# A Perceiver layer on one core: attention in six TensorE runs a group instead of eight, with the last 65 score columns two heads at a time

## The chip, the cores and the metric

The kernel runs on one core of a Trainium2 chip. The metric is the device time of one execution in microseconds; the median of three runs is given. The core has TensorE (matmuls and transposes, written PE in the profile; PEld is its loading of weights), VectorE (DVE), ScalarE (ACT), GpSimd (POOL) and SyncE (SP, which issues DMAs here). TensorE writes to PSUM, eight banks of 128 partitions x 512 words of four bytes; everything else lies in SBUF or in the chip's memory. All numbers are float32.

## The reference, cut to what matters

```python
# x: (16, 64, 1024), ctx_1024: (16, 1601, 256), mask: (64, 1601)
def xattn(q, k, v, mask):             # 32 heads of 32, 8 key/value heads, 4 heads to each
    xq = q.reshape(b, s, 8, 4, 32)
    xk = k.reshape(b, t, 8, 32)
    xv = v.reshape(b, t, 8, 32)
    scores = einsum('bsgrd,btgd->bgrst', xq, xk) / sqrt(32) + mask
    probs = softmax(scores, axis=-1)
    return einsum('bgrst,btgd->bsgrd', probs, xv).reshape(b, s, 1024)

x = x + xattn(layernorm(x), ctx, ctx, mask)
x = x + ffn_half_dropped(layernorm(x), w_gate, w_up, w_down)   # the smaller half of each row of silu(gate) is zeroed
x = x + experts_top2(layernorm(x), router_w, router_b, A, Bm)
```

The context of 1601 rows is both keys and values. The change touches the first of the three steps alone.

## The kernel before, in words

The 1024 rows of `x` are eight tiles of 128 rows (two batches each). The attention of one batch is cut into four groups (`Group(b, h, rh)`: half `h` of the key/value heads, that is four of them, and half `rh` of the four query heads to each). So a group has four heads `g`, one to each 32 partitions of the transposed keys `kT`, and in each head 128 rows (two query heads of 64 rows) against 1601 columns. There are 64 groups, worked off by one loop (`for n in range(ng)`), each in two halves `d`. All engines' instructions keep the order in which the loop issues them; the recorder that sees to it (`InOrder`, line 93) is why every row of the profile says L93, so rows are told apart by their tiles.

A group goes through these steps:

- `scores(c)` (TensorE): for part `c` of the columns, one matmul a head of 32 rows of `kT` with the queries `qt` as weights, into a bank a head (`ps`). The four heads lie in different 32-row strips of TensorE. The parts are `PARTS`: 289, 512, 288 and 512 columns. Heads 0 to 2 write to three banks of their own (`ps_s`), head 3 to one of the four banks of the pool `ps_t` (tag `pt`), which are handed out in rotation and shared with all transposes. A bank is taken anew when its last reader has finished.
- `masked(c)` (VectorE): one instruction a head adds the mask, writes the sum to `sc` in SBUF and leaves the maximum in `mx`; after the last part one reduction makes `nm`, the negated maxima of the four heads. A masked bank is free for the next scores.
- `softmax(g)` (ScalarE): the exponential of a head's 1601 columns, in place, with their sum.
- `turn(heads)` (TensorE): transposes of two heads' probabilities, 13 blocks of up to 128 columns each, four blocks to a bank `pt`; a head gives three banks of four blocks, and the last 65 columns of both heads share a bank, so a turn takes seven banks. `turn` returns the eight copies from `pt` to `pT`: the loop gives the first five to ScalarE, the sixth big one and the two small ones to VectorE.
- `values(c0, c1)` (TensorE): for blocks `c0` to `c1` of the columns, one matmul a head with `v` as weights, summed into one bank `po`; of the group before. `keep` copies `po` to `oT` and takes the reciprocals of the sums.

In a half `d` the loop issues, in this order: scores of a long part (512 columns) of the next group; the turn of two heads of this group; ScalarE's copies; the masks of the long part; VectorE's copies; scores and masks of a short part (288 or 289 columns) of the next group or the one after it; two exponentials; half of the values of the group before (six blocks, then seven). On TensorE each half is four runs of one kind of instruction, a group eight.

Around this stand a few steps that come once in eight groups (`m = n % 8`): the layer norm of the next 128 rows (`Norm.half`, `Norm.end` on VectorE, the power and `scaled_rows`, the normalised rows `xn`, on GpSimd), the turning of its queries (`turn_queries`, TensorE and ScalarE), and of finished outputs (`finish_tile`). GpSimd also makes one of 48 units of weight sums in a group (`sums_made`, `sums_out`, `sums_in`, tile `tw`), which the FFN uses. `load_kv(b + 1)` issues the next batch's keys and values on SP when the second group of batch `b` starts its scores.

Behind the attention the FFN and the experts are ordered by a planner that is not touched.

Of the kernel before, what the change touches and what calls it, by code (L numbers as in the profile page):

```python
# [9 lines left out]
F32 = mybir.dt.float32  # L10
# [6 lines left out]
ALU = mybir.AluOpType  # L17
AX = mybir.AxisListType
PSUM = bass.MemoryType.PSUM

P = 128
B, S, D = 16, 64, 1024
T, C = 1601, 256
HD = 32
NT = B * S // P
NTC = (T + P - 1) // P
TL = T - (NTC - 1) * P

PARTS = [(0, 289), (289, 801), (801, 1089), (1089, T)]
NCH = len(PARTS)  # L30
I = 2752
IC = 344
# [22 lines left out]
def tile_perceiver_layer(  # L55
# [22 lines left out]
    ident = const.tile([P, P], F32, name="ident")  # L78
# [18 lines left out]
    pe, dve, act = InOrder(nc.tensor), InOrder(nc.vector), InOrder(nc.scalar)  # L97
# [27 lines left out]
    early, late = ExitStack(), ExitStack()  # L125

    def new_pool(stack, name, bufs, side="left", space=bass.MemoryType.SB):
        return stack.enter_context(
            tc.tile_pool(name=name, bufs=bufs, side=side, space=space, reuse_waits="tile")
        )  # L130
# [3 lines left out]
    a1 = new_pool(early, "a1", 1)  # L134
    ktp = new_pool(early, "kT", 3)
    qtp = new_pool(early, "qT", 2)
    scp = new_pool(early, "sc", 2)
    xnp = new_pool(late, "xn", 1, "right")
    vp = new_pool(late, "v", 3, "right")
    ptp = new_pool(late, "pT", 8, "right")  # L140
    otp = new_pool(late, "oT", 2, "right")
    twp = new_pool(early, "tw", 3)
    xp = new_pool(late, "x", 3, "right")
# [1 line left out]
    ps_t = new_pool(early, "ps_t", 4, "right", PSUM)  # L145
# [40 lines left out]
    qT, kv, oT, rs_tok = {}, {}, {}, {}  # L186
# [25 lines left out]
    def scaled_rows(i, norm, engine):  # L212

        xn = xnp.tile([P, 2, 4, 4, HD], F32, tag="xn", name=f"xn{i}")
        xv = x[i].rearrange("p (h g r d) -> p h r g d", h=2, g=4, r=4)
        for h in range(2):
            engine.tensor_scalar(
                xn[:, h], xv[:, h], norm.mean, norm.rstd, ALU.subtract, ALU.mult
            )
        return xn  # L220

    def turn_queries(i, xn, h):

        if h == 0:
            qT[i] = qtp.tile([P, 2, 2, 4, S], F32, tag="qt", name=f"qt{i}")
        pt = ps_t.tile([P, 4, P], F32, tag="pt", name=f"ptq{i}_{h}")
        for r in range(4):
            pe.transpose(pt[:, r, :], xn[:, h, r].rearrange("p g d -> p (g d)"), ident)
        act.activation(
            qT[i][:, h].rearrange("p b r s -> p r b s"),  # L230
            pt.rearrange("p r (b s) -> p r b s", b=2),
            AF.Copy, scale=1.0 / math.sqrt(HD),
        )

    class Group:


        def __init__(self, b, h, rh):
            self.b, self.h, self.rh = b, h, rh
            self.name = f"{b}_{h}_{rh}"  # L240
            self.sc, self.pT = {}, {}

        def scores(self, c, spare=False):


            b, h, rh = self.b, self.h, self.rh
            if c == 0:
                self.sc = [
                    scp.tile([P, T], F32, tag=f"sc{g}", name=f"sc{g}_{self.name}")
                    for g in range(4)  # L250
                ]
                self.mx = small.tile([P, 4, NCH], F32, tag="mx", name=f"mx_{self.name}")
                self.sums = small.tile([P, 4], F32, tag="sums", name=f"sums_{self.name}")
                if (h, rh) == (0, 1) and b + 1 < B:
                    load_kv(b + 1)
            t0, t1 = PARTS[c]
            homes = [[(ps_s, f"ps{g}"), (ps_t, "pt")] for g in range(3)]
            homes.append([(ps_t, "pt"), (ps_o, "po")])
            self.ps = []
            for g in range(4):  # L260
                home, tag = homes[g][spare]
                ps = home.tile([P, 512], F32, tag=tag, name=f"ps{g}_{self.name}_{c}")
                self.ps.append(ps)
            for g in range(4):
                rows = slice(g * HD, (g + 1) * HD)
                q = qT[b // 2][rows, h, b % 2, 2 * rh : 2 * rh + 2, :]
                pe.matmul(
                    self.ps[g][:, : t1 - t0],
                    q.rearrange("p r s -> p (r s)"),
                    kv[b][0][h][rows, t0:t1],  # L270
                    start=True,
                    stop=True,
                )

        def masked(self, c, heads=range(4)):


            t0, t1 = PARTS[c]
            for g in heads:
                dve.tensor_tensor_reduce(  # L280
                    out=self.sc[g][:, t0:t1],
                    in0=self.ps[g][:, : t1 - t0],
                    in1=mask2[:, t0:t1],
                    scale=1.0,
                    scalar=LOWEST,
                    op0=ALU.add,
                    op1=ALU.max,
                    accum_out=self.mx[:, g, c : c + 1],
                )
            if c == NCH - 1 and 2 in heads:  # L290
                self.nm = small.tile([P, 4], F32, tag="nm", name=f"nm_{self.name}")
                dve.tensor_reduce(self.nm, self.mx, AX.X, ALU.max, negate=True)

        def softmax(self, g):

# [98 lines left out]
    ng = len(groups)  # L394
# [9 lines left out]
        pe.transpose(warm[:, 0, :], ident, ident)  # L404
    for h in range(2):
        turn_queries(0, xn, h)
    for group, c in [(groups[0], c) for c in range(NCH)] + [(groups[1], c) for c in range(2)]:
        group.scores(c, spare=c % 2 == 1)
        if c % 2 == 0:
            for _ in range(4):  # L410
                pe.transpose(group.ps[3][:, 3 * P :], ident, ident)
        group.masked(c)
    for g in range(2):
        groups[0].softmax(g)

# [2 lines left out]
    for n in range(ng):  # L418
        i, m = n // 8 + 1, n % 8
        group = groups[n]  # L420
        last = n == ng - 1
        if m == 2 and i < NT:
            load_x(i)
        if m == 4 and n > 8:
            sp_queue.dma_start(xs[i - 2], x[i - 2])
        if n == ng - 3:
            for j in range(2):
                x[j] = xp.tile([P, D], F32, tag="x", name=f"x{j}_f")
                sp_queue.dma_start(x[j], xs[j])
        for d in range(2):  # L430
            add = None
            long = (groups[n + 1], 2 * d + 1) if n + 1 < ng and n + d > 0 else None
            short = (groups[n + 1 + d], 2 - 2 * d) if n + 1 + d < ng else None
            if long:
                long[0].scores(long[1])
            if i < NT and d == 1 and m >= 6:
                turn_queries(i, xn, m - 6)
            if n > 8 and 3 <= 2 * m + d <= 4:
                copy, add = finish_tile(i - 2, 1 - d)
                act.copy(*copy)  # L440
            copies = group.turn((2 * d, 2 * d + 1))
            on_act = 3 if last else 5
            for copy in copies[:on_act]:
                act.copy(*copy)
            if long:
                long[0].masked(long[1], (3, 0, 1, 2))
            for copy in copies[on_act:]:
                dve.tensor_copy(*copy)
            if short:
                short[0].scores(short[1])  # L450
                short[0].masked(short[1])
            if d == 0:
                for g in (2, 3):
                    group.softmax(g)
            elif n + 1 < ng:
                for g in range(2):
                    groups[n + 1].softmax(g)
            if add:
                add()
            if n > 0:  # L460
                groups[n - 1].values(*((0, NTC // 2), (NTC // 2, NTC))[d])
                if d == 1:
                    groups[n - 1].keep()
            if i < NT:
                if (m, d) == (4, 0):
                    norm = Norm(x[i], f"q{i}")
                if (m, d) in ((4, 0), (5, 0)):
                    norm.half(m - 4)
                if (m, d) == (5, 1):
                    norm.end()  # L470
                    xn = scaled_rows(i, norm, pool)
            if d == 1 and 0 <= n - 3 < 3 * NU:
                sums_made(n - 3)
                sums_out(n - 3)
            if d == 1 and 0 <= n - 2 < 3 * NU:
                sums_in(n - 2)
            if last:
                xn = first[d].tile([P, D], F32, tag=("xn", "oT")[d], name=f"xn_f{d}")
                norm = Norm(x[d], f"f{d}")
                norm.half(0)  # L480
                norm.half(1)
                norm.end()
                dve.tensor_scalar(xn, x[d], norm.mean, norm.rstd, ALU.subtract, ALU.mult)
                first_xn[d] = xn
# [931 lines left out]
```

## Time and profile before

| | |
|---|---|
| median of three runs | 1723.66 us (1723.62 to 1723.87) |
| the profiled execution's own time | 1721.6 us |
| its span, first to last instruction | 1719.8 us |
| mean granted clock of TensorE | 0.997 |
| the attention's last values start | 837.72 us into the span |
| busy in 200 to 800 us, a group (46.5 groups) | 12.90 us of TensorE |

Busy time of an engine is the union of its instructions' times. A row of a timeline merges neighbours of one kind: it gives the start in us from the span's start, the busy time in us, the engine, what is written and read, the shape, how many instructions, and in brackets the idle time before it and what ended it. TensorE's matmuls overlap in its pipeline, so the time that a run takes is read from its start to the start of the next run, and not from its busy time. A float32 matmul on strips of the array is carried out as two instructions, so eight scores stand in a row for four heads.

### The profile page before, as it was taken

The page shows a single profiled execution, that of the slowest core. Times are in us where ns is not written, and L with a number is a line of the kernel's source. Part 1 is how long each engine was busy: PE and PEld are TensorE (multiplying, and loading weights), DVE is VectorE, ACT ScalarE, POOL GpSimd, SP SyncE. Part 2 cuts the span into 40 slices and gives each one's busy share as a digit, 9 for nine tenths or more (in the row PEclk, how much of TensorE's full clock was granted, in tenths as well). Part 3 has the DMA queues.
Part 4 walks back from the last instruction along what each step waited for, and adds up shares of the span by engine and source line. Part 5 has one row for each costly group of instructions (what it writes and reads, how often), then busy time and mean ns, then how long its engine had stood idle before and what let it go on. Part 6 is the DMA issues. An engine that isn't in the chain of part 4 may idle for free. (4 is left out here: it accounts for less than half of the span.)

```text
span 1719.8 us, 38753 instructions
## 1 busy us (share of the span) xinstructions
PE 1692.3 (98%) x15102; PEld 1151.8 (67%) x15102; DVE 1411.2 (82%) x3655; ACT 1260.8 (73%) x1780; POOL 558.6 (32%) x584
## 2 busy tenths in 40 slices
PE   8999999999999999999999999899999999999999
PEld 6777777777777777777766666446666546645644
DVE  7888888888888888888627999999989999999603
ACT  6999999999999999999544676676737874777010
POOL 2044453454544454110120221512250313332631
PEclk9999999999999999999999999999999999999999
DMA  8236456545556646211599999688989888888873
GB/s 248 85 112 221 144 194 213 186 170 191 172 173 212 204 159 203 70 61 58 193 333 326 307 291 311 210 297 308 301 278 305 266 300 269 285 291 275 317 265 141
DMA packets 132326, 384.56 MB, mean 224 GB/s; under 512 B 9488, under 2 KB 61232, under 8 KB 132144
## 3 DMA queue, kind: packets, MB, share of 16 engines
q1 hardware_dynamic: 113280, 312.83, 55.3%
q0 software_dynamic: 18432, 68.16, 11.7%
q8 instruction: 120, 1.97, 0.5%
q10 hardware_dynamic: 432, 1.09, 0.2%
q14 instruction: 62, 0.51, 0.1%
HBM read 339.58 MB, written 42.47 MB: 222 GB/s over the span
## 5 line engine op out<-in xcount | busy, mean ns | idle before, releaser
L93 DVE CUSTOM_DVE_ANT_0 sc<-ps,mask 128x512 f32<-128x512 f32 (+2 forms) x1024 | 526.3, 571 | 103.1 <-PE ps L93 102.7
L93 ACT ACTIVATE sign<-a,cand 128x2752 int8<-128x2752 f32 x136 | 351.9, 2588 | 107.8 <-DVE cand L93 107.3
L93 ACT ACTIVATE sc<-sc,nm 128x1601 f32<-128x1601 f32 x256 | 420.1, 1666 | 9.6 <-DVE nm L93 9.6
L93 PEld LDWEIGHTS pt<-ident,sc 128*128 128x128 f32 (+1 forms) x3328 | 361.9, 141 | 77.5 <-issue 72.8
L93 PE MATMUL pt<-ident,sc 128*128 128x128 f32 (+1 forms) x3328 | 391.1, 274 | 1.2 <-ACT sc L93 1.1
L93 DVE TENSOR_SCALAR_CACHE_REDUCE junk<-a,cand 128x2752 uint8<-128x2752 f32 x124 | 381.6, 3077 | 3.8
L93 ACT COPY pT<-pt 128x512 f32<-128x512 f32 x636 | 323.8, 607 | 46.2 <-PE pt L93 45.9
L93 PE MATMUL pg_g<-w_g,hS 128*128 128x344 f32 x896 | 263.9, 455 | 6.4 <-DVE s L93 3.3
L93 PE MATMUL pg_u<-w_u,hS 128*128 128x344 f32 x896 | 263.7, 452 | 0.0
L93 POOL TENSOR_TENSOR tw<-tw 128x344 f32<-128x344 f32 (+1 forms) x192 | 176.1, 928 | 267.0 <-DMA tw<-in_wd_dram 89.0
L93 PE MATMUL ps<-kT,qt 32*128 32x512 f32 (+2 forms) x2048 | 247.7, 549 | 3.1 <-DVE mx L93 2.8
L93 PEld LDWEIGHTS pg_g<-w_g,hS 128*128 128x128 f32 x896 | 170.0, 191 | 94.4 <-issue 4.2
L93 PE MATMUL pd<-w_d,s 128*128 128x512 f32 x528 | 231.0, 592 | 0.0
L93 PEld LDWEIGHTS pg_u<-w_u,hS 128*128 128x128 f32 x896 | 168.8, 190 | 86.8 <-issue 3.1
L93 PE MATMUL po<-pT,v 128*32 128x128 f32 x6656 | 208.1, 274 | 0.4 <-ACT oT L93 0.4
L93 PEld LDWEIGHTS po<-pT,v 128*32 128x32 f32 x6656 | 174.1, 110 | 48.6 <-issue 43.7
L93 PEld LDWEIGHTS pd<-w_d,s 128*128 128x128 f32 x528 | 98.6, 190 | 115.3 <-issue 114.8
L93 DVE COPY pT<-pt 65x128 f32<-65x128 f32 (+1 forms) x388 | 141.0, 418 | 23.0 <-PE pt L93 16.0
L93 PEld LDWEIGHTS ps<-kT,qt 32*128 32x128 f32 x2048 | 83.1, 183 | 52.2 <-DVE mx L93 34.8
L93 ACT ACTIVATE s<-s 128x344 f32<-128x344 f32 (+1 forms) x70 | 36.7, 537 | 91.3 <-DVE s L93 90.9
L93 POOL TENSOR_TENSOR s<-s,rank 128x688 f32<-128x688 f32 x32 | 62.4, 1967 | 88.2 <-DVE rank L93 87.4
L93 DVE DVE_READ_ACCUMULATOR2_ANT mx<- 128x1 f32 x1024 | 83.9, 82 | 0.0
(322 smaller groups left out, 1216.5 us busy)
## 6 DMA issues: line engine op xcount, KB each, us to landing
w_g<-ts SPq DMA_DIRECT2D x64, 688.0 KB
w_u<-ts SPq DMA_DIRECT2D x64, 688.0 KB
w_d<-ts SPq DMA_DIRECT2D x48, 768.0 KB
w_g<-in_wg_dram SPq DMA_DIRECT2D x48, 688.0 KB
w_u<-in_wu_dram SPq DMA_DIRECT2D x48, 688.0 KB
w_d<-in_wd_dram SPq DMA_DIRECT2D x36, 768.0 KB
kT<-in_ctx_t_dram SPq DMA_DIRECT2D x31, 800.5 KB
v<-in_ctx_v_dram SPq DMA_DIRECT2D x32, 768.0 KB
```

What stands on the lines that cost most here:

```text
L93: return tc.keep_in_program_order(getattr(self.engine, op)(*args, **kwargs))
```

## The change

The parts become three of 512 columns and one of 65. The 65 columns leave the rhythm of four heads: `rests` scores them two heads at a time, into banks of `ps_t`, just ahead of a 512-column part, so that they lie in the same run on TensorE. The first half of a group scores part 1 of the next group, turns heads 0 and 1, scores the rest of heads 0 and 1 and part 2, and then takes all values of the group before in one run; the second half scores the rest of heads 2 and 3 together with part 0 of the group after the next, and turns heads 2 and 3. TensorE thus has six runs a group. The maxima are reduced for two heads at a time (`maxima`), and the exponentials of the next group start one in each half. In the second half ScalarE gives one more big copy to VectorE (`on_act` is 5, then 4). VectorE masks head 3 first. `sc` gets a third buffer for heads 2 and 3, `pT` goes from eight buffers to six. The layer norm of the next rows and the turning of its queries move to earlier halves.

```diff
--- before.py
+++ after.py
@@ -26,7 +26,7 @@
 NTC = (T + P - 1) // P
 TL = T - (NTC - 1) * P
-PARTS = [(0, 289), (289, 801), (801, 1089), (1089, T)]
+PARTS = [(0, 512), (512, 1024), (1024, 1536), (1536, T)]
 NCH = len(PARTS)
 I = 2752
 IC = 344
@@ -134,10 +134,10 @@
     a1 = new_pool(early, "a1", 1)
     ktp = new_pool(early, "kT", 3)
     qtp = new_pool(early, "qT", 2)
-    scp = new_pool(early, "sc", 2)
+    scp = [new_pool(early, "sc", 2), new_pool(early, "sc_late", 3)]
     xnp = new_pool(late, "xn", 1, "right")
     vp = new_pool(late, "v", 3, "right")
-    ptp = new_pool(late, "pT", 8, "right")
+    ptp = new_pool(late, "pT", 6, "right")
     otp = new_pool(late, "oT", 2, "right")
     twp = new_pool(early, "tw", 3)
     xp = new_pool(late, "x", 3, "right")
@@ -238,22 +238,43 @@
         def __init__(self, b, h, rh):
             self.b, self.h, self.rh = b, h, rh
             self.name = f"{b}_{h}_{rh}"
-            self.sc, self.pT = {}, {}
+            self.sc, self.pT, self.rest = {}, {}, {}
+        def rests(self, heads):
+            for g in heads:
+                self.rest[g] = ps_t.tile(
+                    [P, 512], F32, tag="pt", name=f"rest{g}_{self.name}"
+                )
+                self.product(g, NCH - 1, self.rest[g])
+        def product(self, g, c, out):
+            b, h, rh = self.b, self.h, self.rh
+            t0, t1 = PARTS[c]
+            rows = slice(g * HD, (g + 1) * HD)
+            q = qT[b // 2][rows, h, b % 2, 2 * rh : 2 * rh + 2, :]
+            pe.matmul(
+                out[:, : t1 - t0],
+                q.rearrange("p r s -> p (r s)"),
+                kv[b][0][h][rows, t0:t1],
+                start=True,
+                stop=True,
+            )
         def scores(self, c, spare=False):
             b, h, rh = self.b, self.h, self.rh
             if c == 0:
                 self.sc = [
-                    scp.tile([P, T], F32, tag=f"sc{g}", name=f"sc{g}_{self.name}")
+                    scp[g // 2].tile([P, T], F32, tag=f"sc{g}", name=f"sc{g}_{self.name}")
                     for g in range(4)
                 ]
                 self.mx = small.tile([P, 4, NCH], F32, tag="mx", name=f"mx_{self.name}")
                 self.sums = small.tile([P, 4], F32, tag="sums", name=f"sums_{self.name}")
                 if (h, rh) == (0, 1) and b + 1 < B:
                     load_kv(b + 1)
-            t0, t1 = PARTS[c]
             homes = [[(ps_s, f"ps{g}"), (ps_t, "pt")] for g in range(3)]
             homes.append([(ps_t, "pt"), (ps_o, "po")])
             self.ps = []
@@ -261,25 +282,18 @@
                 home, tag = homes[g][spare]
                 ps = home.tile([P, 512], F32, tag=tag, name=f"ps{g}_{self.name}_{c}")
                 self.ps.append(ps)
             for g in range(4):
-                rows = slice(g * HD, (g + 1) * HD)
-                q = qT[b // 2][rows, h, b % 2, 2 * rh : 2 * rh + 2, :]
-                pe.matmul(
-                    self.ps[g][:, : t1 - t0],
-                    q.rearrange("p r s -> p (r s)"),
-                    kv[b][0][h][rows, t0:t1],
-                    start=True,
-                    stop=True,
-                )
-        def masked(self, c, heads=range(4)):
+                self.product(g, c, self.ps[g])
+        def masked(self, c, heads=(3, 0, 1, 2)):
             t0, t1 = PARTS[c]
             for g in heads:
+                ps = self.rest[g] if c == NCH - 1 else self.ps[g]
                 dve.tensor_tensor_reduce(
                     out=self.sc[g][:, t0:t1],
-                    in0=self.ps[g][:, : t1 - t0],
+                    in0=ps[:, : t1 - t0],
                     in1=mask2[:, t0:t1],
                     scale=1.0,
                     scalar=LOWEST,
@@ -287,9 +301,15 @@
                     op1=ALU.max,
                     accum_out=self.mx[:, g, c : c + 1],
                 )
-            if c == NCH - 1 and 2 in heads:
+        def maxima(self, j):
+            if j == 0:
                 self.nm = small.tile([P, 4], F32, tag="nm", name=f"nm_{self.name}")
-                dve.tensor_reduce(self.nm, self.mx, AX.X, ALU.max, negate=True)
+            heads = slice(2 * j, 2 * j + 2)
+            dve.tensor_reduce(
+                self.nm[:, heads], self.mx[:, heads], AX.X, ALU.max, negate=True
+            )
         def softmax(self, g):
@@ -404,12 +424,19 @@
         pe.transpose(warm[:, 0, :], ident, ident)
     for h in range(2):
         turn_queries(0, xn, h)
-    for group, c in [(groups[0], c) for c in range(NCH)] + [(groups[1], c) for c in range(2)]:
-        group.scores(c, spare=c % 2 == 1)
-        if c % 2 == 0:
-            for _ in range(4):
-                pe.transpose(group.ps[3][:, 3 * P :], ident, ident)
+    for j, (group, c) in enumerate(
+        [(groups[0], c) for c in range(NCH - 1)] + [(groups[1], 0)]
+    ):
+        if j == 2:
+            group.rests((0, 1))
+        group.scores(c, spare=j % 2 == 1)
+        if j == 2:
+            group.rests((2, 3))
         group.masked(c)
+        if j == 2:
+            group.masked(NCH - 1, range(4))
+            for half in range(2):
+                group.maxima(half)
     for g in range(2):
         groups[0].softmax(g)
@@ -427,47 +454,56 @@
             for j in range(2):
                 x[j] = xp.tile([P, D], F32, tag="x", name=f"x{j}_f")
                 sp_queue.dma_start(x[j], xs[j])
+        after = groups[n + 1 : n + 3] + [None, None]
         for d in range(2):
             add = None
-            long = (groups[n + 1], 2 * d + 1) if n + 1 < ng and n + d > 0 else None
-            short = (groups[n + 1 + d], 2 - 2 * d) if n + 1 + d < ng else None
-            if long:
-                long[0].scores(long[1])
-            if i < NT and d == 1 and m >= 6:
+            if i < NT and d == 0 and m >= 6:
                 turn_queries(i, xn, m - 6)
+            ahead, c = (after[0], 1) if d == 0 else (after[1], 0)
+            if d == 1 and after[0]:
+                after[0].rests((2, 3))
+            if ahead:
+                ahead.scores(c)
             if n > 8 and 3 <= 2 * m + d <= 4:
                 copy, add = finish_tile(i - 2, 1 - d)
                 act.copy(*copy)
             copies = group.turn((2 * d, 2 * d + 1))
-            on_act = 3 if last else 5
+            on_act = 3 if last else 5 - d
             for copy in copies[:on_act]:
                 act.copy(*copy)
-            if long:
-                long[0].masked(long[1], (3, 0, 1, 2))
+            if d == 1 and after[0]:
+                after[0].masked(NCH - 1, (2, 3))
+            if ahead:
+                ahead.masked(c)
+            if d == 1 and after[0]:
+                after[0].maxima(1)
             for copy in copies[on_act:]:
                 dve.tensor_copy(*copy)
-            if short:
-                short[0].scores(short[1])
-                short[0].masked(short[1])
             if d == 0:
                 for g in (2, 3):
                     group.softmax(g)
-            elif n + 1 < ng:
-                for g in range(2):
-                    groups[n + 1].softmax(g)
+                if after[0]:
+                    after[0].rests((0, 1))
+                    after[0].scores(2)
+                    after[0].masked(NCH - 1, (0, 1))
+                    after[0].masked(2, (0, 1))
+                    after[0].maxima(0)
+                    after[0].masked(2, (3, 2))
+                if n > 0:
+                    groups[n - 1].values(0, NTC)
+                    groups[n - 1].keep()
+            if after[0]:
+                after[0].softmax(d)
             if add:
                 add()
-            if n > 0:
-                groups[n - 1].values(*((0, NTC // 2), (NTC // 2, NTC))[d])
-                if d == 1:
-                    groups[n - 1].keep()
             if i < NT:
                 if (m, d) == (4, 0):
                     norm = Norm(x[i], f"q{i}")
-                if (m, d) in ((4, 0), (5, 0)):
-                    norm.half(m - 4)
-                if (m, d) == (5, 1):
+                if m == 4:
+                    norm.half(d)
+                if (m, d) == (4, 1):
                     norm.end()
+                if (m, d) == (5, 0):
                     xn = scaled_rows(i, norm, pool)
             if d == 1 and 0 <= n - 3 < 3 * NU:
                 sums_made(n - 3)
```

## The prediction

> **What bounds the kernel now.** I read the page, then the busy time by stretch, then the timelines of TensorE, ScalarE and VectorE over one group of the attention.
>
> ```profile
> core 0: us, PE busy (x) PEld busy (x) DVE busy (x) ACT busy (x) POOL busy (x), PEclk, DMA share, GB/s
> 400.00:600.00 200.00, 200.00 (x2958) 153.08 (x2956) 168.92 (x647) 185.70 (x306) 97.58 (x105) 1.00 0.58 190
> ```
>
> In the steady attention TensorE has no idle time at all, at full clock, while ScalarE (93%) and VectorE (84%) have a little. The chain of waits on the page runs back from the end through the FFN only, so it says nothing of this stage; the timeline does. Its columns are start, busy us, and the run.
>
> ```profile
> 500.12 1.14 PE L93 MATMUL ps<-kT,qt 32*128 32x512 f32 x8
> 501.19 3.06 PE L93 MATMUL pt<-ident,sc 128*128 128x128 f32 x26
> 504.17 0.77 PE L93 MATMUL ps<-kT,qt 32*128 32x289 f32 x8
> 504.87 1.74 PE L93 MATMUL po<-pT,v 128*32 128x128 f32 x56
> 506.54 1.14 PE L93 MATMUL ps<-kT,qt 32*128 32x512 f32 x8
> 507.61 3.06 PE L93 MATMUL pt<-ident,sc 128*128 128x128 f32 x26
> 510.60 0.77 PE L93 MATMUL ps<-kT,qt 32*128 32x288 f32 x8
> 511.30 1.52 PE L93 MATMUL po<-pT,v 128*32 128x128 f32 x48
> ...
> 837.72 3.05 PE L93 MATMUL po<-pT,v 128*32 128x128 f32 x104 [0.39 <-ACT oT L93]
> 840.70 1.09 PE L93 MATMUL pt_f<-ident,xn_f 128*128 128x128 f32 x8
> ```
>
> These are the eight runs of a group, back to back, with no wait between them: from start to start 1.07 + 2.98 + 0.70 + 1.67 + 1.07 + 2.99 + 0.70 + 1.45 = 12.63 us. (200 to 800 us holds 744 instructions of 512 columns, 16 a group, so 46.5 groups and 12.90 us each; the other 0.27 is the turning of queries and outputs.) So TensorE's own work sets the period, and all banks come free in time. How narrowly, the next two show: the copies out of the first turn (501.19), on ScalarE and on VectorE.
>
> ```profile
> 501.94 2.54 ACT L93 COPY pT<-pt 128x512 f32<-128x512 f32 x5 [0.44 <-PE pt L93]
> 504.33 1.67 ACT L93 ACTIVATE sc<-sc,nm 128x1601 f32<-128x1601 f32 x1
> ```
>
> ```profile
> 501.40 0.70 DVE L93 CUSTOM_DVE_ANT_0 sc<-ps,mask 128x512 f32<-128x512 f32 x1 [0.35 <-PE ps L93]
> ...
> 503.24 0.69 DVE L93 CUSTOM_DVE_ANT_0 sc<-ps,mask 128x512 f32<-128x512 f32 x1
> 503.85 0.08 DVE L93 DVE_READ_ACCUMULATOR2_ANT mx<- 128x1 f32 x1
> 503.97 0.17 DVE L93 TENSOR_REDUCE nm<-mx 128x4 f32<-128x16 f32 x1
> 504.06 1.08 DVE L93 COPY pT<-pt 128x512 f32<-128x512 f32 x3
> 505.07 0.46 DVE L93 CUSTOM_DVE_ANT_0 sc<-ps,mask 128x289 f32<-128x289 f32 x1
> ```
>
> The turn ends on TensorE 2.98 after its start. ScalarE's fifth copy ends at 504.48 (3.29 after it), VectorE's copy of the sixth block at 504.06 + 0.69 = 504.75 (3.56 after it; 0.69 is the mean of the 128x512 copies).
>
> **TensorE, part by part.** After the change a group is: scores 512 (1.07), turn (2.98), two 65-column scores and scores 512, values whole, two 65-column scores and scores 512, turn (2.99). Values in one run are shown by the last group, 837.72 to 840.70: 2.98 instead of 1.67 + 1.45 = 3.12. The Trainium skill, "TensorEngine Tiling (Array Packing)", Key Properties, says that changing the tiling mode drains TensorE; this 0.14 is what a saved change is worth here. Without the 65-column pairs that is 3 x 1.07 + 2.98 + 2.99 + 2.98 = 12.16.
>
> No row shows a 65-column pair. A column of a score run costs (1.07 - 0.70) / 223 = 1.66 ns, so 65 of them at least 0.11 us; a run of its own would be 0.70 - 224 x 0.00166 = 0.33. It adds matmuls to a run, so it cannot cost less than nothing. I take the middle, 0.22, since the tiling stays as it is, but weights are loaded for few columns. (The Trainium skill, "TensorE: Matmul & The Clock Gate", LDWEIGHTS, prices a load of 128 columns at 128/1.2 ns whatever its rows; two passes would then make an estimated 0.21 a pair, and 12.58 in place of the 12.60 below.) Two pairs: 12.16 + 0.44 = 12.60, bounds 12.38 and 12.82. Against 12.63 the runs saved and the pairs added nearly cancel.
>
> **The new wait.** The pool of transposed blocks, `pt`, hands out four banks in rotation. After the turn's six blocks and its remainder, before took one more bank (for head 3's scores), which was the fourth block's, long copied. Now three are taken in a row: the pair takes the fourth's and the fifth's, head 3's 512 columns the sixth's. The built order confirms it: the first two wait for ScalarE, the last for VectorE. TensorE arrives at 2.98; the fifth is free at 3.29 and the sixth at 3.56. It takes instructions in order, so the values and all else queue behind. From the later: the run ends 3.56 + 1.07 = 4.63 after the turn's start, where it could end at 2.98 + 0.22 + 1.07 = 4.27, so 0.36; from the earlier: 3.29 + 0.22 + 1.07 = 4.58, so 0.31, beside it. With a hand-over between engines of 0.04 (bounds 0 and 0.19: weight loads of scores waited 23.0 us in 120 times for VectorE, a change of tiling included) I take 0.40, bounds 0.31 and 0.55. The period is 12.60 + 0.40 = 13.00. The pair before the other 512 columns takes banks copied well before.
>
> The Trainium skill's "TensorEngine Tiling (Array Packing)", PSUM Bottleneck, speaks against the change: tiling speeds up TensorE, not the emptying of PSUM. The rows above are that case; by TensorE's own sum alone the change would gain 0.03.
>
> **VectorE.** Masked columns stay 1601 a head; a big copy moves from ScalarE to it (0.61 after overlap: 1.01 for three in the row less two small ones of 0.20), and a second reduction of maxima comes. There is a ring through it: scores of the next-but-one group start, the pair ahead and 1.28 to the first mask (1.50), four masks (2.45), maxima (0.21), two big and two small copies (1.62), four masks of the next set (2.45), the sixth block's copy (0.69), scores into its bank (1.07), values (2.98), and round again: 12.97. So TensorE's sum with the wait and this ring agree at 13.0, and either alone would hold the period above 12.63. Masks of 65 columns lie in VectorE's waits for the 512 behind them: by 1.07 ns a column (689 and 449 ns at 512 and 288) 0.21, at most 0.45 each.
>
> The ring has no slack left, so what else stands in it costs its full time. Of the layer norm of the next rows one half (0.684), the aggregate (0.208) and the addition (0.154) move behind the copies and ahead of the next masks: 1.05 us, in seven of the 64 groups, 7.4 us; bounds 0 and 1.6 each. Before, VectorE's waits for scores (0.35 to 0.95 a half) covered it.
>
> **Edits at nothing.** ScalarE has nine copies at 0.48 (five started in 504.33 - 501.94), four exponentials at 1.62 and a copy at 0.2: 11.0 of 13, so the copy taken from it is no gain on the path. The norm's power goes to GpSimd one group earlier, and a unit of weight sums now stands between it and the normalised rows: 0.57 + 4 x 0.94 + 2 x 0.77 + 2 x 2.07 = 10.0 us from some 2.6 into the sixth group of eight, where the ring has it, so done at 12.6; TensorE turns them after the next scores, at 13.0 + 1.07. That leaves 1.5 of cover, so 0; a unit whose load lands late could eat it, for which I allow 2 us in seven groups. `kT` and `v` are asked for at the same places. At the start 289 columns of masks move into the loop: 0, within 2 us. The FFN is as it was.
>
> **Sum.** 62 full groups x 0.37 = 22.9, and 7.4: 30. The profiled execution has 1721.6 (span 1719.8), the median of the runs is 2.06 above it. 1721.6 + 30 + 2 = 1754.
>
> **Rivals.**
> *Faster or the same: the runs saved come through.* If the fifth and sixth copies end before TensorE arrives, 2.98 after the turn's start, and VectorE's ring is under 12.4, only TensorE's sum is left: pairs at 0.11 give 12.38, 62 x -0.25 = -15.5, 1708; at 0.22 give 12.60, 62 x -0.03 = -2, 1722. For it: a stage that is all TensorE. Against: both copies are in the rows at 3.29 and 3.56, and the sixth block is turned only at 24/26 of the turn, 2.75, and needs 0.69 more: 3.44.
> *Slower still: pairs at the dear end.* 12.82 + 0.55 = 13.37, 62 x 0.74 = 46, and norms at 1.6 (11): 1781 at the outside; 1775 typically. For it: the ring leaves nothing to absorb a surplus.
> *Not what it says:* the built order has six runs a group, so this is out.
>
> **Numbers.** The bank wait and the ring 0.84, slower still 0.07, runs saved 0.09, of which 0.05 faster and 0.04 within 0.2% (3.4 us, about what a measurement can tell from no change). The forecast's own low end: pair at 0.11, hence a ring of 12.86, no price for the norms: 62 x 0.23 = 14, 1738; its high end: wait 0.55 with norms at 1.6: 62 x 0.52 + 11 = 43, 1767. The range goes a little into the dear case: 1738 to 1769. Slower: 0.91.
>
> **What would show it.** Right: TensorE with an idle time of 0.3 to 0.5 in each group ahead of the 65-column or head 3's scores after the first turn, released by ScalarE or VectorE; from 200 to 800 us about 45 groups instead of 46.5; one group in eight over 14 us; values of 2.98 in one run; pairs of 0.22. Wrong: a TensorE without idle time there, with VectorE waiting as before; pairs that cost nothing would shift the sum by 0.44, and a VectorE with idle time ahead of its 512-column masks as long as before would refute the ring.

## The result and the profile after

The change made the kernel slower: 1753.78 us median of four runs (1751.02 to 1756.03) beside 1723.64 for the kernel before on the same chip, a ratio of 1.0178 (1.0165 to 1.0190). The forecast was 1754.0 within 1738 to 1769. Two of the four runs took 1756.0 at a mean granted clock of 0.993 over the whole execution, the other two 1751.0 and 1751.6 at 0.996, so the median lies between two levels. The profiled execution took 1756.03 with a span of 1754.3, so it is the longest of the four, against 1721.6 and 1719.8 before; differences between the two profiles are therefore a little larger than between the medians.

First, busy time by stretch in the steady attention.

```profile
core 0: us, PE busy (x) PEld busy (x) DVE busy (x) ACT busy (x) POOL busy (x), PEclk, DMA share, GB/s
400.00:600.00 200.00, 198.87 (x2850) 154.83 (x2849) 174.30 (x654) 173.33 (x278) 96.25 (x104) 1.00 0.58 182
```

TensorE did 2850 matmuls here instead of 2958, at the same full clock, and still counts as busy for 99% of the time. Busy time alone would not show the loss. The timeline of TensorE over one group does (start, busy us, the run):

```profile
503.87 1.14 PE L93 MATMUL ps<-kT,qt 32*128 32x512 f32 x8
504.94 3.06 PE L93 MATMUL pt<-ident,sc 128*128 128x128 f32 x26
507.93 0.68 PE L93 MATMUL rest<-kT,qt 32*128 32x65 f32 x3
508.29 0.70 PE L93 MATMUL ps<-kT,qt 32*128 32x512 f32 x2
508.45 0.27 PE L93 MATMUL rest<-kT,qt 32*128 32x65 f32 x1
508.56 1.13 PE L93 MATMUL ps<-kT,qt 32*128 32x512 f32 x6
509.61 3.05 PE L93 MATMUL po<-pT,v 128*32 128x128 f32 x104
512.59 0.33 PE L93 MATMUL rest<-kT,qt 32*128 32x65 f32 x2
...
512.86 1.08 PE L93 MATMUL ps<-kT,qt 32*128 32x512 f32 x6
513.87 3.06 PE L93 MATMUL pt<-ident,sc 128*128 128x128 f32 x26
516.86 1.14 PE L93 MATMUL ps<-kT,qt 32*128 32x512 f32 x8
517.93 1.53 PE L93 MATMUL pt<-ident,sc 128*128 128x128 f32 x12
519.97 1.72 PE L93 MATMUL pt<-ident,sc 128*128 128x128 f32 x14 [0.50 <-DVE mx L93]
```

Read it from start to start. From 503.87 to 516.86 a group takes 12.99 (13.00 in most), where before had 12.63. The pair and its 512 columns behind the values take 1.28 (512.59 to 513.87). The same work behind the first turn takes 1.68 (507.93 to 509.61). That 0.40 is the bank wait. It has no idle time of its own in the timeline: the rows of the pair and of the 512 columns count as busy while some of their instructions wait. What the pair and head 3 wait for stands in the timelines of ScalarE and VectorE:

```profile
505.69 2.54 ACT L93 COPY pT<-pt 128x512 f32<-128x512 f32 x5 [0.39 <-PE pt L93]
```

```profile
505.15 0.69 DVE L93 CUSTOM_DVE_ANT_0 sc<-ps,mask 128x512 f32<-128x512 f32 x1
...
506.99 0.69 DVE L93 CUSTOM_DVE_ANT_0 sc<-ps,mask 128x512 f32<-128x512 f32 x1
...
507.82 1.08 DVE L93 COPY pT<-pt 128x512 f32<-128x512 f32 x3
...
516.51 1.67 DVE L93 COPY pT<-pt 128x512 f32<-128x512 f32 x4
518.11 0.68 DVE L93 BATCH_NORM_STATS2 st_q<-x 128x6 f32<-128x512 f32 x1
518.82 0.21 DVE L93 BATCH_NORM_AGGREGATE mv_q<-st_q 128x2 f32<-128x12 f32 x1
519.06 0.15 DVE L93 TENSOR_SCALAR ve_q<-mv_q 128x1 f32<-128x1 f32 x1
519.13 0.68 DVE L93 CUSTOM_DVE_ANT_0 sc<-ps,mask 128x512 f32<-128x512 f32 x1
...
520.96 0.69 DVE L93 CUSTOM_DVE_ANT_0 sc<-ps,mask 128x512 f32<-128x512 f32 x1
...
521.57 1.08 DVE L93 COPY pT<-pt 128x512 f32<-128x512 f32 x3
```

The turn began at 504.94. ScalarE's fifth copy ends at 508.23, 3.29 behind that, and VectorE's first copy, the sixth block, at 507.82 + 0.69 = 508.51, 3.57 behind it. TensorE stood ready at 2.99. Its rows of 512 columns start at 508.29 and 508.56, 0.06 and 0.05 behind the ends of these two copies, and 1.05 behind the later of these rows the run ends, 4.67 behind the turn's start.

VectorE itself was not late for that. Behind a set of masks it can go on 0.61 after its last mask has started (520.96 and 521.57, in the group with a norm). In the regular group the last mask starts at 506.99, so it stood ready at 507.60, and its copy of the sixth block starts at 507.82, 0.22 later, when TensorE has turned that block (504.94 + 2.75 = 507.69).

In the group with a norm, 1.02 us of the norm lie between the copies and head 3's mask (518.11 to 519.13). The turn needs that mask's bank, waits 0.50, and ends later. In 200 to 800 us there are six such waits, one in each eight groups.

**Where the time went.** The last group's values start at 872.10 instead of 837.72, 34.4 later, and behind them the FFN takes 882.2 instead of 882.1. The 34.4 are worked out from the starts of the values runs. Eight groups take 106.63 instead of 102.80, 0.479 a group more. The 61 groups from the first values to the one before the last two take 811.70 instead of 783.08, so 28.6 more. The last two groups give back 1.4 (16.45 instead of 17.86). The first values start at 43.95 instead of 36.78, 7.2 later: 28.6 - 1.4 + 7.2 = 34.4. Of the 7.2, 1.0 is no loss of the start, since the run ahead of the values holds more (1.68 instead of 0.70); that leaves 6.2 for the start and 28.2 for the groups. In the start, by busy time and granted clock (columns as above), first before, then after:

```profile
0.00:40.00 40.00, 34.53 (x272) 24.56 (x273) 28.72 (x106) 22.88 (x35) 12.54 (x21) 0.96 0.88 266
```

```profile
0.00:40.00 40.00, 31.96 (x171) 22.63 (x172) 25.26 (x90) 17.08 (x25) 7.37 (x15) 0.79 0.79 231
```

The clock is 0.79 of full speed instead of 0.96. TensorE's timeline in the start of after says what came ahead of that:

```profile
8.13 2.00 PE L93 MATMUL ps<-kT,qt 32*128 32x512 f32 x16 [0.18 <-ACT qt L93]
14.03 0.48 PE L93 MATMUL rest<-kT,qt 32*128 32x65 f32 x2 [3.90 <-DMA kT<-in_ctx_t_dram]
```

It waits 3.90 us for keys: the 65 left-over columns are the last of them, and the change asks for them before the third part of 512. The transposes that before put between its first sets to keep TensorE at work are not in the changed kernel either.

### The profile page after: what moved, and what is told of

Its sections match the earlier page's. It is cut to its first block, busy times and chain, and to the rows that moved or that the text cites. A ratio compares the mean times of both kernels' runs of the same rounds, so it can differ in the third digit from the quotient of the medians.

```text
span 1754.3 us, 38531 instructions
## 1 busy us (share of the span) xinstructions
PE 1720.3 (98%) x15090; PEld 1186.3 (68%) x15090; DVE 1459.1 (83%) x3782; ACT 1238.4 (71%) x1717; POOL 557.6 (32%) x584
## 4 chain that ended last, share of the span: by engine, by line
PE 74%; DVE 19%; issue 3%; ACT 2%; DMA 1%; POOL 0%; SPq 0%; DVEq 0%; ACTq 0%; POOLq 0%
PE pt L93 20%; PE pg_g L93 12%; PE ps L93 11%; PE po L93 11%; PE pg_u L93 10%; DVE junk L93 10%; PE pd L93 4%; PE rest L93 3%; DVE rank L93 2%; DVE sc L93 1%; DVE pT L93 1%; ACT sign L93 1%; DMA w_g<-ts 1%; PE py L93 1%; DVE cand L93 1%
## 5 line engine op out<-in xcount | busy, mean ns | idle before, releaser
L93 DVE CUSTOM_DVE_ANT_0 sc<-ps,mask 128x512 f32<-128x512 f32 x768 | 488.8, 687 | 65.2 <-PE ps L93 62.3
L93 PE MATMUL pt<-ident,sc 128*128 128x128 f32 (+1 forms) x3328 | 395.4, 276 | 3.9 <-DVE mx L93 3.5
L93 ACT COPY pT<-pt 128x512 f32<-128x512 f32 x573 | 293.8, 605 | 31.6 <-PE pt L93 31.1
L93 PE MATMUL ps<-kT,qt 32*128 32x512 f32 x1536 | 253.9, 642 | 1.9 <-DVE mx L93 1.8
L93 PEld LDWEIGHTS po<-pT,v 128*32 128x32 f32 x6656 | 177.9, 110 | 47.4 <-issue 47.4
L93 PE MATMUL po<-pT,v 128*32 128x128 f32 x6656 | 195.1, 274 | 0.0
L93 DVE COPY pT<-pt 65x128 f32<-65x128 f32 (+1 forms) x451 | 178.1, 453 | 17.0 <-PE pt L93 10.8
L93 PEld LDWEIGHTS ps<-kT,qt 32*128 32x128 f32 x1536 | 92.3, 186 | 15.1 <-issue 8.9
```

The costliest lines, as they stand in the source:

```text
L93: return tc.keep_in_program_order(getattr(self.engine, op)(*args, **kwargs))
```

## The experiments

The theory is that of the forecast: the pair takes the fourth's and fifth's blocks' banks and head 3's 512 columns the sixth's, so TensorE waits for the copies (0.4 a group), and the norm stands in VectorE's way. Its rival from the forecast is the ring: VectorE's own work would hold the period near 13.0 whatever TensorE does. A third suspect came with the profile after: the start.

**The pair behind the 512 columns.** The pair's scores move behind the 512 columns, and its masks behind two of theirs, so that head 3's 512 columns have the fourth block's bank, as before, and the pair the later two, needed 1.07 us later.

```diff
-                    after[0].rests((0, 1))
                     after[0].scores(2)
-                    after[0].masked(NCH - 1, (0, 1))
+                    after[0].rests((0, 1))
                     after[0].masked(2, (0, 1))
+                    after[0].masked(NCH - 1, (0, 1))
                     after[0].maxima(0)
```

> The changed kernel, with the 65-column pair of heads 0 and 1 issued behind the 512 columns of its run instead of ahead of them, on TensorE and on VectorE. Bank theory (TensorE waits in front of the pair and of head 3's scores for the copies of the fifth and sixth blocks): head 3's columns now take the fourth block's bank, and the pair meets its two banks while TensorE is still busy with the 512 columns; the regular group falls from 13.00 to TensorE's own 12.55 to 12.60 us, no idle time ahead of the run, the whole to 1724 to 1729. Rival, the VectorE ring: the ring loses only the 512 columns behind the sixth copy and would stand near 12.1, so the same; this run does not tell it from the bank theory. Rival, pairs that cost more than assumed wherever they stand: no change, 1754.

Measured: 1723.62 us, 1.0009 (0.9999 to 1.0018) of the kernel before, 30.2 us less than the changed kernel; a loss clear of noise is not left. TensorE's timeline:

```profile
488.26 3.06 PE L93 MATMUL pt<-ident,sc 128*128 128x128 f32 x26
491.25 1.14 PE L93 MATMUL ps<-kT,qt 32*128 32x512 f32 x8
492.21 0.33 PE L93 MATMUL rest<-kT,qt 32*128 32x65 f32 x4
492.48 3.05 PE L93 MATMUL po<-pT,v 128*32 128x128 f32 x104
```

The run takes 1.23 (491.25 to 492.48) instead of 1.68, and the regular group 12.53, below before's 12.63. VectorE and ScalarE do as much as before this edit. The list of waits would have misled here: weight loads of 65-column scores wait 9.1 us in 41 times for ScalarE in 200 to 800 us, and 7.3 us in 41 times in the changed kernel, so this entry does not measure the bank wait. But the forecast's ring ran through the sixth block's bank too, so this run settles that the bank costs the time, and not yet whether VectorE holds the period beside it. The pair behind the 512 columns costs 1.23 - 1.07 = 0.16, ahead of them 0.21. The gain of 0.10 a regular group does not show in the total, since the norm's group still has 13.23 and eight groups 102.87.

**The pair between head 3's 512 columns and the other three.** All three banks are still taken in one run, but in another order: head 3 takes the fourth's, the pair the fifth's and sixth's, and three products of 512 columns stand behind them.

```diff
...
-            for g in range(4):
+            for g in (3, 0, 1, 2) if rests else range(4):
                 self.product(g, c, self.ps[g])
+                if g == 3:
+                    self.rests(rests)
...
-                    after[0].rests((0, 1))
-                    after[0].scores(2)
+                    after[0].scores(2, rests=(0, 1))
```

> The changed kernel, with the same instructions in the same run, but head 3's 512 columns issued first, then the pair, then heads 0 to 2: head 3 takes the fourth block's bank and the pair those of the fifth and sixth. Bank theory: the pair's second head waits for VectorE's copy of the sixth block, and three heads' 512 columns stand behind it, so the run ends 3.60 + 0.22 + 1.07 = 4.89 us after the turn's start instead of 4.67; regular group 13.2, the whole 13 to 14 us slower, about 1767. Rival, pairs that cost more than assumed: no change, 1754, since the work is the same.

Measured: 1769.06 us, 1.0263 (1.0246 to 1.0281); 15.3 more than the changed kernel.

```profile
500.90 0.69 PE L93 MATMUL ps<-kT,qt 32*128 32x512 f32 x1
501.25 0.43 PE L93 MATMUL rest<-kT,qt 32*128 32x65 f32 x2
...
502.81 3.05 PE L93 MATMUL po<-pT,v 128*32 128x128 f32 x104
```

The run takes 1.91 (500.90 to 502.81) instead of 1.68, the regular group 13.22 instead of 13.00, with the same work on every engine. More work behind the awaited bank costs more, so the wait for the bank sets the end of this run. Beside the first experiment this shows the bank wait from both sides.

**The copy back on ScalarE.** The change moved one big copy to VectorE; this moves it back. It takes 0.61 us out of VectorE's ring and leaves the bank wait.

```diff
-            on_act = 3 if last else 5 - d
+            on_act = 3 if last else 5
```

> The changed kernel, with ScalarE making five of the six big copies in both halves again, which takes 0.61 us a group from VectorE. Bank theory: the regular group stays at 13.00, because TensorE waits for a block that is turned late and not for a busy VectorE; only the group with the layer norm gets shorter by some 0.4, so 3 us in all, 1751. Rival, the VectorE ring is the bound: the regular group falls by up to 0.4, 1729 to 1735.

Measured: 1752.83 us, 1.0171 (1.0156 to 1.0187), not separated from the changed kernel's 1.0178 by the intervals.

```profile
503.13 0.68 PE L93 MATMUL rest<-kT,qt 32*128 32x65 f32 x3
...
504.81 3.05 PE L93 MATMUL po<-pT,v 128*32 128x128 f32 x104
...
513.13 1.53 PE L93 MATMUL pt<-ident,sc 128*128 128x128 f32 x12
514.82 1.72 PE L93 MATMUL pt<-ident,sc 128*128 128x128 f32 x14 [0.16 <-DVE mx L93]
```

The run that waits still takes 1.68, and the regular group 12.99. VectorE's work does not set the period. The group with the norm falls from 13.75 to 13.41 and its wait from 0.50 to 0.16: there VectorE does count.

**The norm where VectorE waits for scores.** Its two halves and its end go to the first halves of the fourth and fifth group of eight (`m` 3 and 4), where VectorE waits for scores; so none of it stands behind the copies of a second half.

```diff
-                if (m, d) == (4, 0):
+                if (m, d) == (3, 0):
                     norm = Norm(x[i], f"q{i}")
-                if m == 4:
-                    norm.half(d)
-                if (m, d) == (4, 1):
+                if (m, d) in ((3, 0), (4, 0)):
+                    norm.half(m - 3)
+                if (m, d) == (4, 0):
                     norm.end()
```

> The changed kernel, with the layer norm's two halves and its end in the first halves of the fourth and fifth group of eight, where VectorE waits for scores, instead of behind its copies. Ring theory: the norm's 1.05 us no longer stands ahead of masks, the longest group of eight loses 0.8 to 1.1, 6 to 8 us in all, 1747. Rival, the group is long because of GpSimd's normalised rows or the turning of queries: no change, 1754.

Measured: the norm's group falls from 13.75 to 12.99, as the regular one. That is 0.76 in seven groups, 5.3 us, a little under what was expected. The median, 1751.27 or 1.0158 (1.0143 to 1.0173), lies only 2.5 below the changed kernel's, and the intervals overlap, so the 5.3 is read from the groups and not from the total. In the two profiles the last values start 8.6 apart (863.48 and 872.10): 5.25 of it lies in the groups and 3.37 in the start, which this edit does not touch (first values at 40.58 and 43.95).

**The start, in two steps.** First the order alone: the left-over columns behind all four products of the third part.

```diff
-        if j == 2:
-            group.rests((0, 1))
         group.scores(c, spare=j % 2 == 1)
         if j == 2:
-            group.rests((2, 3))
+            group.rests(range(4))
```

> The changed kernel; at the start alone, the first group's 65-column scores (whose keys are the last to land) stand behind its third 512-column part on TensorE, not ahead. Theory that the start costs because this wait for the keys holds up the third part and VectorE with it: the first values start 1 to 2 us earlier than 43.9, and the whole falls by as much, to about 1752. Rival, the third part's own keys land as late: no change. The regular group stays at 13.00 by every theory.

Measured: 1753.72 us, 1.0176 (1.0161 to 1.0191): nothing in the median. Its clock in the first 40 us was 0.83, its first values at 41.46. TensorE waits 0.76 for keys ahead of the third part instead of 3.90 ahead of the left-over columns. The profile does not show what the order is worth either: the five other kernels that start in the changed kernel's order (the pair behind, the pair between, the copy back, the norm moved, and the one without the start's two steps below) had clocks of 0.79 to 0.87 and first values from 40.58 to 43.35.

The start thus differs from execution to execution. After and the kernel with the norm moved do the same work there; one stretch with its clock, and the turn in it, first after, then the other:

```profile
31.00:37.00 6.00, 6.00 (x23) 4.50 (x24) 2.74 (x11) 2.86 (x6) 0.00 (x0) 0.50 0.71 224
...
32.91 5.37 PE L93 MATMUL pt<-ident,sc 128*128 128x128 f32 x26
```

```profile
31.00:37.00 6.00, 6.00 (x48) 4.31 (x47) 5.06 (x18) 4.62 (x9) 0.00 (x0) 1.00 0.70 220
...
31.84 3.06 PE L93 MATMUL pt<-ident,sc 128*128 128x128 f32 x26
```

Until 30.9 us the two differ by 0.12, at the first values by 3.37. So some 3.3 of after's 6.2 belong to a second stretch at half clock that the one execution had and the other had not.

The second step adds transposes ahead of the third and fourth sets, to keep TensorE at work while it waits for keys:

```diff
...
+            for _ in range(fill):
+                pe.transpose(self.ps[3][:, :P], ident, ident)
             for g in range(4):
                 self.product(g, c, self.ps[g])
...
-        group.scores(c, spare=j % 2 == 1)
+        group.scores(c, spare=j % 2 == 1, fill=(0, 0, 32, 16)[j])
```

> The changed kernel with the order at the start of the run before, and 32 and 16 filling transposes (without use) ahead of the third and fourth set of scores, as the kernel before had 4 behind every other set. Clock theory (the start of the changed kernel runs at a halved clock for 10.2 and 6.8 us, since TensorE has nothing to do while keys land): the halved stretches shrink to one of 3.4 as before, the first values start at 37 to 40, 3 to 6 us off the whole, 1748 to 1751. Rival, the start is set by masks and by the keys' landing: the clock stays full, and the first values start no earlier than without the fill.

Measured: 1751.92 us, 1.0162 (1.0145 to 1.0178). The stretch of the start:

```profile
0.00:40.00 40.00, 36.73 (x334) 27.79 (x337) 30.91 (x112) 22.68 (x33) 7.42 (x15) 1.00 0.78 231
```

Full clock throughout, and the first values at 37.77, ahead of all that start without the transposes. The median is just above what was expected, and the medians of the two steps are 1.8 apart with overlapping intervals. So what the transposes do to the clock of the start is shown; what that is worth in the median is not.

**All three mended**, that is, the pair behind, the norm moved, the start in order and with transposes.

> Pair behind the 512 columns, layer norm in VectorE's waits, filling transposes at the start, all three in the changed kernel. If the three causes are all, eight groups take 4 x 12.53 + 13.4 + 2 x 13.05 + 12.6 = 102.2 us (before 102.8), 5 us less in 62 groups than the run with the pair behind alone, and 3 less at the start: 1714 to 1719, 0.2 to 0.5% below the kernel before. If the clock at the start is no cause: 1718 to 1720. If something else is lost: no lower than 1722.

Measured: 1718.81 us, 0.9974 (0.9964 to 0.9984), the first version that beats both kernels. Its regular groups and the one with the norm take 12.53, eight groups 102.16. In a second set of runs the same kernel stood beside one without the start's two steps:

> All three mends once more, beside the run without the mended start, on the same chip: 1717 to 1720, 0.1 to 0.4% below the kernel before, first values at 37 to 40, at most one halved stretch of 3.4 in the first 40 us.

> Pair behind the 512 columns and layer norm in VectorE's waits, but the start of the changed kernel: no filling transposes, and the first group's 65 columns ahead of its third part. Clock theory: two halved stretches of some 10 and 7 us in the first 40 us again, first values 3 to 5 us later than with the mended start, the whole 2 to 5 us slower than the run with all three beside it, 1720 to 1723. Rival, the start hardly counts because later waits absorb it: equal within 1 us.

Measured: 1718.27, 0.9970 (0.9958 to 0.9983), with the transposes, and 1720.33, 0.9981 (0.9971 to 0.9990), without, at clocks of 0.96 and 0.83 in the first 40 us and first values at 39.05 and 42.16. This time 2.1 in favour of the transposes, again with overlapping intervals.

**Values in one run alone.** The kernel before, with its own parts of 289, 512, 288 and 512 columns, but the values of a group in one run.

```diff
-                groups[n - 1].values(*((0, NTC // 2), (NTC // 2, NTC))[d])
-                if d == 1:
+                if d == 0:
+                    groups[n - 1].values(0, NTC)
```

> The kernel before with one part of the change alone: all values of a group in one run, in its first half; parts, pairs and everything else as before. By the number of runs alone it saves 0.14 us a group, 9 us in all, 1714. Bank theory: without values between them, the second half's 288 or 289 columns and the next 512 stand next to each other, and the 512 wait for the masks to empty the three banks of heads 0 to 2: the third is free about 1.4 us after the short scores' end; 62 x 1.3 gives about 80 us more, 1800.

Measured: 1809.12 us, 1.0496 (1.0480 to 1.0512), a little above what was expected.

```profile
508.67 3.06 PE L93 MATMUL pt<-ident,sc 128*128 128x128 f32 x26
511.66 0.77 PE L93 MATMUL ps<-kT,qt 32*128 32x289 f32 x8
513.07 2.05 PE L93 MATMUL ps<-kT,qt 32*128 32x512 f32 x8 [0.64 <-DVE mx L93]
```

With no values between them, the 512 columns behind the 289 start 1.41 after these instead of 0.70 and wait for masks; a regular group takes 13.95. The half run of values that the change removes was also the cover for VectorE's masks. So the parts of 512 and the whole run of values belong together; the slowdown comes from the third edit, where the left-over columns were put.

## Why the prediction was right, step by step

- **TensorE's own sum**, 12.60: right, and its parts too. Values in one run take 2.98 (509.61 to 512.59). The pair ahead of 512 columns costs 1.28 - 1.07 = 0.21 for a forecast 0.22 (bounds 0.11 and 0.33). That is also what the Trainium skill, "TensorE: Matmul & The Clock Gate", LDWEIGHTS, gave as an estimate; behind the 512 columns the same pair costs 0.16, where a price by columns loaded does not know the order. The one saved run is worth 3.12 - 2.98 = 0.14, as forecast; that this is the drain of a changed tiling mode ("TensorEngine Tiling (Array Packing)", Key Properties) is not shown by a run of its own.
- **The bank wait**, 0.40, for a regular group of 13.00: right in place, mechanism and size. The copies end at 3.29 and 3.57 (forecast 3.29 and 3.56), the run 4.67 behind the turn's start (forecast 4.63 + 0.04), the group is 13.00. Taking the wait away gave 12.53, more work behind it 13.22.
- **VectorE's ring**, 12.97: a step that failed without harm. By its sum, 0.61 less on VectorE makes a ring of 12.36; the group stayed at 12.99, so the ring is not what holds it. The claim that the ring has no slack failed by some 0.2: VectorE stood ready 0.22 ahead of the sixth block's copy, which by an estimate makes the ring 12.99 - 0.22 = 12.77. That it alone would still hold the period above 12.63 is not tested: the edit that took the wait away took 1.07 of scores out of the ring as well. In the sum the error cost nothing, because the ring was not added to the wait.
- **The norm**, 1.05 in seven groups: right in place, too big in size: 0.75 (13.75 instead of 13.00), 5.3 us instead of 7.4. In its group the next masks start 0.99 late (519.13 instead of 505.15 + 12.99 = 518.14); less the 0.22 of slack that is 0.77.
- **The start**, priced at 0 within 2: failed. It looked at the masks alone. It overlooked that the keys' last 65 columns are now needed first, that the transposes between the first sets go, and so that TensorE waits 3.90 us and the clock falls to 0.79. In the profiled run the start costs 6.2 us, and 2.8 in the kernel with the norm moved, whose start is the same. How the cost divides between the wait and the clock stays open.
- **The turning of queries**, which moves to first halves, had no price in the forecast. It takes 0.51 in each of two groups (13.51) instead of 0.44 (13.07 before), so 0.14 in eight groups. The turning of outputs takes 0.87 in one group (13.87), as before (13.50).
- **The sum**, 30: in the profiled run the groups came to 28.2 instead of 30.3, and the start to 6.2 instead of 0. Two errors of opposite sign lie in the 1754.0. And no run of the four came closer than 2.2 to the median of 1753.78, which lies between two levels. So the closeness to it is luck; that the loss is near 30 is not.
- **The signs.** 45 groups in 200 to 800 us: 600/(106.63/8) = 45.0, as said. An idle time of 0.3 to 0.5 in each group: the wait is there, but as a longer run and not as idle time; by idle time alone one would have called the forecast refuted. One group in eight over 14 us: none, the norm's is 13.75, and the longest, with outputs, 13.87. A VectorE that waits as long as before ahead of its 512-column masks: 42.1 us in 45 groups instead of 75.0 in 46.5 (with 22.9 more ahead of the pair's masks), so this sign did not refute the ring.

## What to carry to other kernels

When a change puts more tiles through a pool that hands out its buffers in rotation, write down for each new tile which buffer it gets, who reads that buffer last and when, before counting what the instructions cost; here moving two small scores behind four large ones was worth 30 us of 1754. Measure a run from its start to the start of the next, since a wait inside a run can pass as busy time. And look at what else an edit removes: the half run of values covered VectorE's masks, the early transposes kept TensorE at work in the start.

## What was not expected of the hardware

TensorE can lose 3% of a stage and count as 99% busy: 198.87 of 200 us, while 0.40 of each 13.00 was a wait. The same 65-column pair costs 0.21 ahead of four matmuls of 512 columns and 0.16 behind them.

The granted clock of the start differed between executions of the same work, and not only between kernels: over the first 40 us it was 0.79 to 0.87 in six profiles with the changed kernel's order, 0.83 with the order mended, 0.96 in before and 0.96 to 1.00 with transposes in the wait. The Trainium skill, "TensorE: Matmul & The Clock Gate", Why this matters for your kernels, says that about 3 us without matmuls bring the clock back to half; after agrees with that, with 0.50 granted from 14 to 24 us behind its wait of 3.90 us. Its second stretch at 0.50, from 31 to 37 us, has no such wait ahead of it (0.17 and 0.29 us since 23 us), and what set it off stays open. That stretch is worth some 3.3 us between two profiles; between kernels with and without the transposes the medians differ by 1.8 and 2.1 us, with overlapping intervals.
